# The last batch of a two-layer graph network: denominators by products, a new order on GpSimd, and an end row block by block

## The chip, the cores and the metric

One core of a Trainium2 chip (trn2) runs the whole program. The metric is the device time of one execution in microseconds (us). The kernel before took 3909.1 us, the median of three runs (3908.46 to 3909.31). The traces name the engines PE (TensorE, matrix products), PEld (its weight loads), DVE (VectorE), ACT (ScalarE), POOL (GpSimd) and SP (SyncE, which issues the transfers).

The change acts on the last 90 us of some 3904 us, so a time of one execution is a blunt tool: it also holds the luck of everything earlier. So beside the times I use three stretches of each trace:

- **start to sums**: from the start of the last batch's first scores product to the end of its last denominator product;
- **sums to statistic**: from there to the end of the last row's statistics on VectorE;
- **closing**: from there to the end of the span.

## The reference, cut to what matters

Two layers over 32 batches of 512 nodes with 512 features: a graph sum with layer norm, then masked attention with 8 heads of 64, an output projection and layer norm.

```python
x = _layernorm(x + _L0_gnn_ref(x, adj, W, b))                 # layer 0
q, k, v = split_heads(x @ Wq.T + bq), ...                     # layer 1
scores = jnp.where(adj == 0, -inf, einsum('bhqd,bhkd->bhqk', q, k) / 8)
attn = softmax(scores)                                        # divides by the row's sum: the denominator
out = einsum('bhqk,bhkd->bhqd', attn, v)
x = _layernorm(x + out @ Wo.T + bo)
```

## The kernel before

Batches are pipelined. Attention of batch b runs in eight steps, counted from 0 to 7 below, two for each of four pairs of heads; into each step the program puts pieces of other work (projections of batch b - 1, the next batch's layer 0). Each engine works through its own list in program order. For the last batch there is no next batch, so the steps are thin and waits show.

```python
def presum(hp, half):          # denominators: add the four blocks of masked exponentials
    if half == 0:
        ES[hp] = work([P, 2, N], "es", 1)
        nc.gpsimd.tensor_add(ES[hp], E[0], E[1])
    else:
        nc.vector.tensor_add(ES[hp], ES[hp], E[half])        # half = 2, 3: 1.22 us each or more

def sums(b, hp):               # then one product with ones for each head
    pl = ov_tile()
    for s in range(2):
        nc.tensor.matmul(pl[s*HD:(s+1)*HD, :], ones[:, :HD], ES[hp][:, s, :], start=True, stop=True)
    RL[hp] = (pl, work([P, N], "rl", 1))

def rest(b, hp):               # four reciprocals, scaling of the pair's values, a checksum (the "told sum")
    return [(invert, b, hp, c) for c in range(4)] + [(scale, b, hp), (tell, b, hp)]

def last_steps():              # the work put into the last batch's eight steps
    m = B - 2
    p = [pc("pj", m, i, bank) for i, bank in ALONE]          # seven pieces of m's output projection: 1,6,2,7,5,4,3
    c = [z(combos, TO, m, ot_quarter(m), (1, 2)), z(combos, TO, m, ot_quarter(m), (3, 4))]
    own = [(4 * GA, last_part, hp, 0) for hp in range(3)]    # the last batch's own projection, blocks 0 and 1
    return [[z(last_load), p[0], FLUSH] + c + [z(add_bo, B-1, 0), z(add_bo, B-1, 1)], [p[1], p[2]], [p[3], p[4]],
            [p[5], p[6], z(stats, m, 0), z(stats, m, 1)],
            [FLUSH, own[0], z(apply, m, 0), z(apply, m, 1), z(store, m)], [own[1]], [FLUSH, own[2]], []]

def last_part(hp, half):
    if hp == 0:
        if half == 0: ACC[0], ACC[1] = mm_tile("a"), mm_tile("b")
        else:
            t = sc_tile()
            ACC[2], ACC[3] = t[:, 0, :], t[:, 1, :]          # two halves of ONE tile
    ...                                                       # one product for each block of 128 rows

# the end row, after the eight steps
values(B - 1, HP - 1, 1)
sums(B - 1, HP - 1)
for hp in range(HP - 1): last_part(hp, 1)                     # blocks 2 and 3, pairs 0 to 2
for g in rest(B - 1, HP - 1): ...                             # reciprocals, scaling
for ic in range(2): last_part(HP - 1, ic)
tell(B - 1, HP - 1)
for ic in range(NC): last_rows(ic)                            # add, statistics, normalise, store
```

FLUSH means: issue here what is left of `rest`. Piece 1 leaves three additions for GpSimd; the combinations (differences of quarters of the attention's result) are GpSimd's too, and pieces 5, 6, 7 and 4 read them. A "piece" waits for its combination, and the values of one pair wait for the scaling of an earlier pair, which frees their PSUM buffer (a tile that holds results of TensorE). The masks, of which the texts speak, are VectorE's multiplications of the exponentials by the graph's edges.

## Time and profile before

| part of the trace of before | from | to | us |
|---|---|---|---|
| all that the change leaves alone | 0 | 3804.28 | 3804.28 |
| start to sums | 3804.28 | 3881.98 | 77.70 |
| sums to statistic | 3881.98 | 3894.41 | 12.43 |
| closing | 3894.41 | 3904.1 | 9.69 |

Only the last three rows can move. TensorE's waits in them are 0.47, 5.00, 2.17, 2.98, 4.22 and 1.40 us; the prediction shows the lines of the four longest. A trace line gives start, length, engine, line of the program, operation, output and inputs, shapes, and in square brackets the idle time ahead of it with what ended it.

### The profile page before, as it was taken

The numbers are of one execution on the slowest core, as the hardware profiler recorded it, in microseconds if no ns is written. First come the engines' busy times: TensorE is split into PE (matmuls) and PEld (weight loads), VectorE is DVE, ScalarE is ACT, GpSimd is POOL, SyncE is SP. The second block draws the span as 40 slices with busy tenths as digits, with TensorE's granted clock in tenths as the row PEclk, the third lists the DMA queues.
The fourth block names the chain that finished last, engine by engine and source line by source line (L and its number), as shares of the span: only waits on it lengthen the run. The fifth ranks groups of instructions, "written<-read, shape, count | busy, mean of one in ns | idle before, by whom it ended". The sixth has DMA issues, their size and how long they took to land.

```text
span 3904.1 us, 46897 instructions
## 1 busy us (share of the span) xinstructions
PE 3848.6 (99%) x17370; PEld 2639.9 (68%) x17370; DVE 2606.6 (67%) x3525; ACT 1057.8 (27%) x1476; POOL 1900.3 (49%) x1861
## 2 busy tenths in 40 slices
PE   9999999999999999999999999999999999999997
PEld 6666666766676666676667676667666667666763
DVE  4667676666666676666767666666667666666666
ACT  2222222222222222322222222222222232222222
POOL 4455554554544545445555355454454544555523
PEclk9999999999999999999999999999999999999998
DMA  7333333333334233333333332333433333333330
GB/s 251 116 109 100 114 108 116 120 91 110 114 108 124 87 116 111 111 119 111 97 114 110 114 122 90 111 113 109 123 90 113 114 108 120 114 95 112 111 106 23
DMA packets 281866, 433.88 MB, mean 111 GB/s; under 512 B 23072, under 2 KB 119840, under 8 KB 281632
## 3 DMA queue, kind: packets, MB, share of 16 engines
q1 hardware_dynamic: 281376, 430.27, 35.5%
q8 instruction: 142, 2.33, 0.2%
q14 instruction: 92, 0.75, 0.1%
q0 software_dynamic: 256, 0.53, 0.0%
HBM read 389.29 MB, written 41.42 MB: 110 GB/s over the span
## 4 chain that ended last, share of the span: by engine, by line
PE 76%; DVE 12%; POOL 9%; issue 2%; ACT 1%; DMA 0%; SPq 0%; POOLq 0%
PE mma L375 22%; PE mmb L375 22%; PE sc L427 10%; PE ov L448 9%; POOL xh L390 5%; PE mmb L299 3%; DVE rl L461 3%; PE mma L299 3%; PE ov L455 2%; DVE st L265 2%; DVE xh L393 2%; POOL big L344 2%; DVE e L432 2%; POOL es L438 2%; PE sc L292 2%
## 5 line engine op out<-in xcount | busy, mean ns | idle before, releaser
L432 DVE TENSOR_TENSOR e<-sc,edge 128x1024 f32<-128x1024 f32 x512 | 602.5, 1218 | 421.8 <-ACT sc L431 421.8
L431 ACT ACTIVATE sc<-sc 128x1024 f32<-128x1024 f32 x512 | 493.1, 1007 | 1276.0 <-PE sc L427 1275.7
L375 PE MATMUL mmb<-ring,big 128*128 128x256 f32 x3144 | 733.6, 382 | 8.2 <-POOL big L344 7.9
L375 PE MATMUL mma<-ring,big 128*128 128x256 f32 x3112 | 725.2, 381 | 4.3 <-POOL big L344 3.0
L375 PEld LDWEIGHTS mmb<-ring,big 128*128 128x128 f32 x3144 | 591.6, 190 | 131.9 <-DVE e L432 23.5
L375 PEld LDWEIGHTS mma<-ring,big 128*128 128x128 f32 x3112 | 583.9, 190 | 129.4 <-DVE e L432 25.2
L344 POOL TENSOR_TENSOR big<-big 128x512 f32<-128x512 f32 x376 | 549.5, 1488 | 220.1 <-DVE big L293 177.9
L184 POOL TENSOR_TENSOR xlo<-xh,xhi 128x512 fp32r<-128x512 f32 x128 | 200.6, 1577 | 738.2 <-ACT xhi L183 738.2
L427 PE MATMUL sc<-q,k 64*128 64x512 f32 x2048 | 509.7, 616 | 0.0
L448 PE MATMUL ov<-e,v 128*64 128x512 f32 x2048 | 497.1, 606 | 8.2 <-DVE oT L471 8.2
L461 DVE RECIPROCAL rl<-ov 128x128 f32<-128x128 f32 x512 | 462.6, 930 | 5.6 <-PE ov L455 1.8
L375 PE MATMUL mma<-big,ring 128*128 128x256 f32 x1808 | 433.1, 382 | 2.2 <-DVE xh L393 2.2
L375 PE MATMUL mmb<-big,ring 128*128 128x256 f32 x1776 | 425.3, 382 | 3.1 <-DVE xh L393 2.4
L267 POOL TENSOR_SCALAR mv<-mv 128x1 f32<-128x1 f32 x256 | 50.4, 197 | 740.5 <-DVE mv L266 730.4
L375 PEld LDWEIGHTS mma<-big,ring 128*128 128x128 f32 x1808 | 337.9, 190 | 80.6 <-issue 26.0
L438 POOL TENSOR_TENSOR es<-e 128x1024 f32<-128x1024 f32 x128 | 301.3, 2354 | 173.6 <-PE ov L455 172.3
L375 PEld LDWEIGHTS mmb<-big,ring 128*128 128x128 f32 x1776 | 332.0, 190 | 78.7 <-issue 24.3
L448 PEld LDWEIGHTS ov<-e,v 128*64 128x64 f32 x2048 | 124.7, 136 | 349.2 <-issue 274.2
L440 DVE TENSOR_TENSOR es<-es,e 128x1024 f32<-128x1024 f32 x256 | 353.4, 1380 | 0.1
L427 PEld LDWEIGHTS sc<-q,k 64*128 64x128 f32 x2048 | 176.5, 186 | 208.9 <-issue 207.0
L393 DVE TENSOR_TENSOR xh<-xh,mmb 128x512 f32<-128x512 f32 x186 | 125.8, 677 | 211.8 <-PE mmb L375 210.7
L390 POOL TENSOR_TENSOR xh<-xh,p 128x512 f32<-128x512 f32 x186 | 231.9, 1275 | 72.4 <-ACT sc L431 39.0
(141 smaller groups left out, 3688.1 us busy)
## 6 DMA issues: line engine op xcount, KB each, us to landing
ring<-wq SPq DMA_DIRECT2D x160, 256.0 KB, 2.6
ring<-wv SPq DMA_DIRECT2D x160, 256.0 KB, 2.6
ring<-wk SPq DMA_DIRECT2D x160, 256.0 KB, 5.4
ring<-wi SPq DMA_DIRECT2D x155, 256.0 KB, 2.6
ring<-wj SPq DMA_DIRECT2D x155, 256.0 KB, 2.7
ring<-wo SPq DMA_DIRECT2D x155, 256.0 KB, 2.6
xh<-in_x_dram SPq DMA_DIRECT2D x32, 1024.0 KB, 6.6
out_dram<-xh SPq DMA_DIRECT2D x31, 1024.0 KB, 5.2
```

Source lines behind the costliest of these rows:

```text
L299: nc.tensor.matmul(pm, parts[w][:, jc, :], adjR[:, jc, :], start=(w == 0 and jc == 0), stop=(w == 1 and jc == NC - 1))
L344: nc.gpsimd.tensor_tensor(dst, p, q, op=OP.subtract)
L375: nc.tensor.matmul(pm[:, c * Q:(c + 1) * Q], lhs, rhs, start=first, stop=(kc == 1 and n == len(terms) - 1), skip_group_check=True)
L390: nc.gpsimd.tensor_tensor(d, d, p1, op=OP.add)
L393: nc.vector.tensor_tensor(d, d, pm, op=OP.add)
L427: nc.tensor.matmul(ps[:, s, :], KT[b, hp // 2][r, hp % 2, kc * P:(kc + 1) * P], QT[b, hp // 2][r, hp % 2, :], start=True, stop=True)
L431: nc.scalar.activation(ps, ps, AF.Exp, scale=QSCALE)
L432: nc.vector.tensor_tensor(e, ps, edge[:, kc:kc + 1, :].to_broadcast([P, 2, N]), op=OP.mult)
L438: nc.gpsimd.tensor_add(ES[hp], E[0], E[1])
L440: nc.vector.tensor_add(ES[hp], ES[hp], E[half])
L448: nc.tensor.matmul(PV[hp][s * HD:(s + 1) * HD, :], V[b][:, kc, c0:c0 + HD], E[kc][:, s, :], start=(kc == 0), stop=(kc == NC - 1))
L461: nc.vector.reciprocal(rl[:, c], pl[:, c])
```

## The change

The intent, in three parts. **Order:** in the first step of the last batch, the denominator sum and the first combinations go ahead of the additions on GpSimd, piece 2 ahead of piece 6. **Products:** in the last batch, TensorE multiplies three things by ones and accumulates, so VectorE's two additions for each pair go away. **End row:** reciprocal, scaling and projection go block by block, with each block's row behind them.

```diff
+    def last_sums(hp, parts=(0, 2, 3)):
+        if 0 in parts:
+            RL[hp] = (ov_tile(), work([P, N], "rl", 1))
+        for kc in parts:
+            src = ES[hp] if kc == 0 else E[kc]
+            for s in range(2):
+                nc.tensor.matmul(RL[hp][0][s*HD:(s+1)*HD, :], ones[:, :HD], src[:, s, :], start=(kc == 0), stop=(kc == 3))
 ...
-        return [[z(last_load), p[0], FLUSH] + c + [z(add_bo, B-1, 0), z(add_bo, B-1, 1)], [p[1], p[2]], [p[3], p[4]], [p[5], p[6], z(stats, m, 0), z(stats, m, 1)],
-                [FLUSH, own[0], z(apply, m, 0), z(apply, m, 1), z(store, m)], [own[1]], [FLUSH, own[2]], []]
+        return [[z(last_load), FLUSH, c[0], p[1], c[1]], [p[2], p[6]], [p[5], p[7], z(add_bo, B-1, 0), z(add_bo, B-1, 1)],
+                [p[3], p[4], z(stats, m, 0), z(stats, m, 1)], [FLUSH, own[0], z(apply, m, 0), z(apply, m, 1), z(store, m)],
+                [own[1]], [FLUSH, own[2]], []]
 ...
-                    sums(b, ph)
+                    last_sums(ph) if b == B - 1 else sums(b, ph)
 ...
-            late = [(presum, hp, 0)] if half == 0 else [(presum, hp, 2), (presum, hp, 3)]
+            late = [(presum, hp, 0)] if half == 0 else [(presum, hp, 2), (presum, hp, 3)] if b < B - 1 else []
 ...
-    values(B - 1, HP - 1, 1)
-    sums(B - 1, HP - 1)
+    last_sums(HP - 1, (0,))
+    for kc in (2, 3):
+        values(B - 1, HP - 1, 1, (kc,))
+        last_sums(HP - 1, (kc,))
     for hp in range(HP - 1):
         last_part(hp, 1)
-    for g in rest(B - 1, HP - 1): ...
-    for ic in range(2):
-        last_part(HP - 1, ic)
+    for ic in range(NC):
+        invert(B - 1, HP - 1, ic)
+        scale(B - 1, HP - 1, slice(ic * P, (ic + 1) * P))
+        last_part(HP - 1, ic=ic)
+        if ic > 0:
+            last_rows(ic - 1)
     tell(B - 1, HP - 1)
-    for ic in range(NC):
-        last_rows(ic)
+    last_rows(NC - 1)
```

In the new list `p` is keyed by the piece's own number.

More of the change, by code (lines that the diff above doesn't have):

```diff
@@ L440, in presum, with values @@
             nc.vector.tensor_add(ES[hp], ES[hp], E[half])
-    def values(b, hp, half):
+    def values(b, hp, half, kcs=None):
         if half == 0:
             PV[hp] = ov_tile()
-        for kc in range(2 * half, 2 * half + 2):
+        for kc in kcs or range(2 * half, 2 * half + 2):
             for s in range(2):
@@ L456, in sums @@
         RL[hp] = (pl, work([P, N], "rl", 1))
+    def last_sums(hp, parts=(0, 2, 3)):
[4 more added lines that the diff above has]
+            for s in range(2):
+                nc.tensor.matmul(RL[hp][0][s * HD:(s + 1) * HD, :], ones[:, :HD], src[:, s, :], start=(kc == 0), stop=(kc == 3))
     def invert(b, hp, part):
@@ L466, in tell, with scale @@
         nc.vector.tensor_tensor_reduce(pl, pl, rl, 1.0, 0.0, OP.add, OP.add, told[:, j:j + 1])
-    def scale(b, hp):
+    def scale(b, hp, c=slice(0, N)):
         if hp % 2 == 0:
             OT[b, hp // 2] = work([P, 2, N], "oT", 3)
-        nc.vector.tensor_mul(OT[b, hp // 2][:, hp % 2, :], PV[hp], RL[hp][1])
+        nc.vector.tensor_mul(OT[b, hp // 2][:, hp % 2, c], PV[hp][:, c], RL[hp][1][:, c])
     def rest(b, hp):
@@ L634, in last_steps @@
         m = B - 2
-        p = [pc("pj", m, i, bank) for i, bank in ALONE]
+        p = {i: pc("pj", m, i, bank) for i, bank in ALONE}
         c = [z(combos, TO, m, ot_quarter(m), (1, 2)), z(combos, TO, m, ot_quarter(m), (3, 4))]
         own = [(4 * GA, last_part, hp, 0) for hp in range(3)]
-        return [[z(last_load), p[0], FLUSH] + c + [z(add_bo, B - 1, 0), z(add_bo, B - 1, 1)], [p[1], p[2]], [p[3], p[4]], [p[5], p[6], z(stats, m, 0), z(stats, m, 1)],
-                [FLUSH, own[0], z(apply, m, 0), z(apply, m, 1), z(store, m)], [own[1]], [FLUSH, own[2]], []]
+        return [[z(last_load), FLUSH, c[0], p[1], c[1]], [p[2], p[6]], [p[5], p[7], z(add_bo, B - 1, 0), z(add_bo, B - 1, 1)],
+                [p[3], p[4], z(stats, m, 0), z(stats, m, 1)], [FLUSH, own[0], z(apply, m, 0), z(apply, m, 1), z(store, m)],
+                [own[1]], [FLUSH, own[2]], []]
     def run(f):
@@ L649, in last_load, with last_part @@
         W["wo"] = [t[:, 0:2, :], t[:, 2:4, :]]
-    def last_part(hp, half):
+    def last_part(hp, half=None, ic=None):
         if hp == 0:
@@ L657, in last_part @@
                 ACC[2], ACC[3] = t[:, 0, :], t[:, 1, :]
-        for ic in range(2 * half, 2 * half + 2):
+        for ic in (range(2 * half, 2 * half + 2) if ic is None else (ic,)):
             nc.tensor.matmul(ACC[ic], OT[B - 1, hp // 2][:, hp % 2, ic * P:(ic + 1) * P], W["wo"][hp // 2][:, hp % 2, :],
@@ L723, in gnn_attention_kernel @@
             extra = []
-    values(B - 1, HP - 1, 1)
-    sums(B - 1, HP - 1)
+    last_sums(HP - 1, (0,))
+    for kc in (2, 3):
+        values(B - 1, HP - 1, 1, (kc,))
+        last_sums(HP - 1, (kc,))
     for hp in range(HP - 1):
         last_part(hp, 1)
-    for g in rest(B - 1, HP - 1):
-        if g[0] is not tell:
-            g[0](*g[1:])
-    for ic in range(2):
-        last_part(HP - 1, ic)
+    for ic in range(NC):
[4 more added lines that the diff above has]
+            last_rows(ic - 1)
     tell(B - 1, HP - 1)
-    for ic in range(NC):
-        last_rows(ic)
+    last_rows(NC - 1)
     flags()
```

## The prediction

> **What bounds the kernel now.** I read the page first: engines, clock row, chain of waits. All of it is one core running 32 batches.
>
> ```profile
> PE 3848.6 (99%) x17370; PEld 2639.9 (68%) x17370; DVE 2606.6 (67%) x3525; ACT 1057.8 (27%) x1476; POOL 1900.3 (49%) x1861
> PEclk9999999999999999999999999999999999999998
> ```
>
> TensorE is busy for 99% of the span and its clock falls in the last fortieth only. The diff acts on the last batch only (its conditions are `b == B - 1`, or code after the loop; the last period's list is its own), so nothing before about 3808 us of the 3904.1 us span should move. Ninety-odd us are in play, 2.4% of the span, and most of those are products that stay. Next I read that stretch as a timeline, by engine, and in windows. First its opening:
>
> ```profile
> 3811.62 3.72 POOL L390 TENSOR_TENSOR xh<-xh,p 128x512 f32<-128x512 f32 x3 [27.32 <-ACT p L382]
> 3815.31 2.33 POOL L438 TENSOR_TENSOR es<-e 128x1024 f32<-128x1024 f32 x1
> 3817.61 1.25 POOL L344 TENSOR_TENSOR big<-oT 128x512 f32<-128x512 f32 x1
> 3818.94 1.26 POOL L344 TENSOR_TENSOR big<-oT,big 128x512 f32<-128x512 f32 x1
> ...
> 3820.25 3.67 PE L375 MATMUL mmb<-ring,big 128*128 128x256 f32 x8 [5.00 <-POOL big L344]
> ```
>
> GpSimd works through three additions, a denominator sum and two combinations, in program order. Piece 6 of the output projection needs the second combination, so TensorE stands for 5.00 us, then runs its eight instructions in 3.67 us where the same group elsewhere takes 1.92. The windows (columns: stretch, its length, then busy time of PE, PEld, DVE, ACT, POOL, then clock, DMA share, GB/s) give the reason:
>
> ```profile
> 3820.00:3822.00 2.00, 1.75 (x4) 1.48 (x5) 0.00 (x0) 0.00 (x0) 2.00 (x3) 0.57 0.00 0
> 3834.00:3838.00 4.00, 1.86 (x8) 0.56 (x9) 3.96 (x6) 1.93 (x2) 0.00 (x0) 1.00 0.00 0
> 3855.00:3857.00 2.00, 1.90 (x6) 0.76 (x8) 2.00 (x4) 0.00 (x0) 0.00 (x0) 0.50 0.48 178
> 3870.00:3872.00 2.00, 2.00 (x4) 0.66 (x2) 0.00 (x0) 0.00 (x0) 0.00 (x0) 0.50 0.00 0
> ```
>
> After idle gaps of 5.00, 2.98 and 4.22 us the clock is half; after one of 2.17 us (in the second line) it is whole. The gaps come from one chain, here in TensorE's timeline with its idle time in brackets:
>
> ```profile
> 3838.03 1.94 PE L448 MATMUL ov<-e,v 128*64 128x512 f32 x8 [2.17 <-DVE oT L471]
> ...
> 3855.10 3.26 PE L448 MATMUL ov<-e,v 128*64 128x512 f32 x8 [2.98 <-DVE oT L471]
> ...
> 3869.14 2.07 PE L659 MATMUL mma<-xh,oT 128*128 128x512 f32 x2 [4.22 <-DVE oT L471]
> ```
>
> Sums on TensorE, then four reciprocals and the scaling on VectorE, then TensorE may go on. The end, from the chain of waits (start, length, what):
>
> ```profile
> 3879.53 1.23 DVE es L440
> 3880.77 0.14 issue
> 3880.90 1.08 PE ov L455 x4
> 3881.98 5.35 PE sc L659 x12
> 3887.33 0.87 PE mma L659 x2
> 3888.20 0.02 issue
> 3888.23 0.70 DVE xh L664
> ```
>
> From 3888.23 VectorE does four rows back to back; its last statistic ends at 3894.42. Small GpSimd operations, one activation, a store and the closing instructions fill the rest to 3904.1. VectorE's reciprocals (`L461`) are hidden behind the twelve products.
>
> **What the Trainium skill says.** "TensorE: Matmul & The Clock Gate", part 1: clock gated to half after an idle window of about 3.4 us, windows free-running. The trace agrees: the clock returns at about 3823.7, 3857.8 and 3874.9 (worked out from the means of my windows), which are 10 and 5 times 3.41 us apart. A window 33% busy lowered it (3851.0 to 3854.4), one 57% busy did not (3833.9 to 3837.3). "TensorEngine Tiling (Array Packing)", When to Use Tiling: with 64 columns of stationary operand two products share the array. It fits: two 128*64 sums over 512 columns take 0.86 to 0.88 us together, one 128*128 product over 512 columns 0.87 us alone. "VectorE: DVE Perf Modes", First, the fixed hardware budget: reciprocal is an iterated divide. The trace agrees that it is dear: 0.85 us for 128 columns in a run of four, as against 0.69 us for a multiplication over 512.
>
> **The change, part by part.** I lay the measured durations along the new program order. Units from the chain: scores 1.92, values 1.87, one product of the sums for a pair of heads 0.86, two pieces 1.92 + 1.74, an own pair 1.92, sums' end to scaled result seen by TensorE 4.20 (3.40 reciprocals, 0.70 scaling, waits 0.10). All starts below drop the 3800.
>
> 1. Order on GpSimd. The denominator sum now starts when its inputs and buffer are there (about 9.1), ends at 11.4; the first combination ends 12.7; the second waits for VectorE's scaling (ends 13.2) and ends 14.5; the three additions follow to 18.2. TensorE: values 13.31 to 15.18, piece 2 (wants only the scaled heads), piece 6, both done at 18.84, 2.5 us behind GpSimd. Before, they were done at 25.65. Gain 6.8: 5.0 of wait and 1.75 of half clock. The bias addition, 6.93 us, moves a step later, where GpSimd has nothing else.
>
> 2. Three products for one, step 2: two more at 0.86, cost 1.7. Shift 5.1.
>
> 3. Step 3 waits for the scaling as before. On VectorE the order (piece, reciprocal, piece, three reciprocals, scaling) is the same, so the 2.17 us gap stays: 0.
>
> 4. Step 4 costs another 1.7, but here VectorE was late: sums done at 48.3, reciprocals only at 50.84, because two additions at 1.22 us, the statistics and the masks were in its queue. Without the additions its masks end at 38.58 + 0.6 (piece) + 3.3 (statistics) + 2.3 (masks) = 44.8, TensorE's sums at 44.9. Values of step 5 start at 44.92 + 4.20 = 49.1, before 55.10. Shift 6.0, so this step gives 0.9 net. TensorE's own pair and scores fill to 48.7: a gap of 0.5 for 2.98.
>
> 5. With that gap gone the clock stays: 1.87 for 3.26. Gain 1.4, shift 7.4.
>
> 6. Step 6: 1.7 more of products, the gap of 4.2 stays, and the half clock behind it. Shift 5.65: values of step 7 at 70.2 for 75.82.
>
> 7. Last pair of heads: values 1.87, then five groups of four instructions at about 0.87, sums done at 76.4 (28 instructions, no wait). Before: 81.98, with 2.47 of additions in the way. The masks end at about 72.8, ahead of their use. Shift 5.6.
>
> 8. End row. The twelve products of the first three pairs are still ahead of the last pair's in TensorE's order, so the first row can be added no sooner than 6.25 after the sums (3888.23 less 3881.98), as before. In that wait VectorE now does only two blocks of reciprocal and scaling (2.4); then it stands at row 0, in order. Blocks 2 and 3 (0.87 + 0.30 each; the 0.30 is an estimate from 0.28 for a 128-column operation on VectorE) and the told sum (0.75) come between the rows. From first addition to last statistic: 1.63 + 3 x 1.52 + 2 x 1.17 + 0.75 = 9.3, before 6.19. Loss 3.1.
>
> Sum: 6.8 - 1.7 + 0 + (2.6 - 1.7) + 1.4 - 1.7 - 0.1 - 3.1 = 2.5 us gained. The closing stretch is unchanged. 3909.1 - 2.5 = 3906.6.
>
> **The rivals.** (a) The block-by-block end pays as intended: then the 5.6 of point 7 survive, perhaps with a us more, 3902.5 to 3903.5. Against it: the twelve products hold the first row, and VectorE had idle time there which it now spends waiting in order; for it only that the stores start earlier and spread out. (b) The products cost more than they free: 6.9 us more of TensorE, and the first wait only moves to another operation (the additions, now late on GpSimd, holding VectorE's addition of piece 6). Then 3909 to 3911. Against it: piece 6 needs only the first addition, done at 15.8, and comes at 18.8. (c) The clock falls in another place. The gap of step 3 was just short of it; with the windows otherwise placed a gap of 2.2 lies all in one window of 3.41 with some 40 to 50% chance (an estimate from the 33 and 57% above), costing up to 1.7. Where the gap of step 6 lies decides whether half clock lasts one window or two: 1.2 either way. This is luck for each execution: 3905 to 3908.5.
>
> **Range and chances.** I take 3906.6. Luck of the windows is plus or minus 1.5, the end row plus or minus 1, so 3904.8 to 3908.3 eight times in ten, with rival (a) the likelier miss. All rivals are within 0.2% of the time before; 2% is 78 us, more than the stretch's waits together. Faster by 2%: 0.005, within 2%: 0.99, slower: 0.005.
>
> **What would show it.** Right: piece 2 straight behind the values near 3815, no wait for GpSimd's combination, clock whole there; step 5's wait under 1 us and its values at 1.9; twelve instructions for the sums at 2.6; a VectorE wait of about 3.5 between the second scaling and the first row's addition, then reciprocals between the rows and 9.3 us to the last statistic. Wrong: a new long wait in steps 1 to 3, half clock behind step 3, or a last statistic less than 7.5 us after the first row's addition.

## The result, and the profile after

The changed kernel took 3904.77 us, the median of four runs (3903.31 to 3906.64); before, with one run more, 3908.78 (3904.76 to 3909.31). The ratio is 0.9992, 95% interval 0.9975 to 1.001. By that interval the two cannot be told apart by their times alone. The traces can: the span went from 3904.1 to 3901.5 us, and the parts are

| part | before | after | gain | foretold |
|---|---|---|---|---|
| up to the last batch | 3804.28 | 3803.72 | 0.56 | 0 |
| start to sums | 77.70 | 72.02 | 5.68 | 5.6 |
| sums to statistic | 12.43 | 17.68 | -5.25 | -3.1 |
| closing | 9.69 | 8.08 | 1.61 | 0 |

The whole page hardly changes; its first line, which answers to the one of before, shows only 32 more matrix instructions:

```profile
PE 3853.7 (99%) x17402; PEld 2641.4 (68%) x17402; DVE 2595.7 (67%) x3520; ACT 1057.0 (27%) x1476; POOL 1909.7 (49%) x1861
```

The opening of the last batch in the timeline of after, GpSimd first, then TensorE:

```profile
3808.52 2.35 POOL L438 TENSOR_TENSOR es<-e 128x1024 f32<-128x1024 f32 x1 [24.79 <-PE ov L455]
3810.83 1.27 POOL L344 TENSOR_TENSOR big<-oT 128x512 f32<-128x512 f32 x1
3812.74 1.28 POOL L344 TENSOR_TENSOR big<-oT,big 128x512 f32<-128x512 f32 x1 [0.64 <-DVE oT L480]
3813.97 3.74 POOL L390 TENSOR_TENSOR xh<-xh,p 128x512 f32<-128x512 f32 x3
...
3825.38 4.95 POOL L326 TENSOR_TENSOR xh<-xh,bo_r 128x512 f32<-128x512 f32 x4
```

```profile
3812.74 1.94 PE L448 MATMUL ov<-e,v 128*64 128x512 f32 x8 [0.47 <-DVE oT L480]
3814.61 1.99 PE L375 MATMUL mma<-ring,oT 128*128 128x256 f32 x8
3816.44 1.89 PE L375 MATMUL mmb<-ring,big 128*128 128x256 f32 x8
```

Piece 2 and piece 6 follow the values without a bracket, so without a wait, and both take 1.9 us: whole clock. The second combination starts when VectorE's scaling is there and ends at 3814.0, 2.4 us ahead of its use. The waits that were 2.17, 2.98 and 4.22 us are now:

```profile
3832.43 1.94 PE L448 MATMUL ov<-e,v 128*64 128x512 f32 x8 [2.17 <-DVE oT L480]
...
3848.69 1.94 PE L448 MATMUL ov<-e,v 128*64 128x512 f32 x8 [0.48 <-DVE oT L480]
...
3863.12 2.08 PE L669 MATMUL mma<-xh,oT 128*128 128x512 f32 x2 [4.22 <-DVE oT L480]
```

The middle one has gone with the half clock behind it (3.26 us before, 1.94 now). Then the end row, VectorE and TensorE:

```profile
3877.97 0.29 DVE L480 TENSOR_TENSOR oT<-ov,rl 128x128 f32<-128x128 f32 x1
3881.98 0.69 DVE L674 TENSOR_TENSOR xh<-xh,mma 128x512 f32<-128x512 f32 x1 [3.72 <-PE mma L669]
...
3887.20 0.29 DVE L480 TENSOR_TENSOR oT<-ov,rl 128x128 f32<-128x128 f32 x1
3889.65 0.69 DVE L674 TENSOR_TENSOR xh<-xh,sc 128x512 f32<-128x512 f32 x1 [2.17 <-PE sc L669]
```

```profile
3884.84 1.48 PE L669 MATMUL sc<-xh,oT 128*128 128x512 f32 x2 [2.04 <-DVE oT L480]
3887.54 2.08 PE L669 MATMUL sc<-xh,oT 128*128 128x512 f32 x2 [1.22 <-DVE oT L480]
```

VectorE stands 3.72 us at row 0, as the prediction said, and then again 2.17 us at row 2, as it did not. Row 2's own product began at 3884.84 and was long done at 3889.65; what ended just then (3887.54 + 2.08) is the product of block 3. The two blocks are halves of one tile. Block 3's product ran at half clock (the granted clock was 0.50 from 3886 to 3890): 2.08 us, where a product at whole clock takes 1.02. Last, the closing stretch. SyncE's waits, before and after (who waited for whom, us in total, times, longest):

```profile
SPq L869 <- PEq L869: 2.3, 2, 2.0
```

```profile
SPq L881 <- PEq L881: 0.4, 2, 0.2
```

The closing barriers of the program wait 2.0 us for TensorE's instruction stream in one kernel and not in the other, though no line of the closing code was touched.

### The profile page after: what moved, and what is told of

It reads as the page before. It is cut to its first block, busy times and chain, and to the rows that moved or that the text cites. A ratio compares the mean times of both kernels' runs of the same rounds, so it can differ in the third digit from the quotient of the medians.

```text
span 3901.5 us, 46958 instructions
## 1 busy us (share of the span) xinstructions
PE 3853.7 (99%) x17402; PEld 2641.4 (68%) x17402; DVE 2595.7 (67%) x3520; ACT 1057.0 (27%) x1476; POOL 1909.7 (49%) x1861
## 4 chain that ended last, share of the span: by engine, by line
PE 77%; DVE 12%; POOL 8%; issue 2%; ACT 1%; DMA 0%; SPq 0%
PE mma L375 23%; PE mmb L375 23%; PE sc L427 10%; PE ov L448 9%; POOL xh L390 5%; PE mmb L299 3%; DVE rl L470 3%; PE mma L299 3%; PE ov L455 2%; DVE xh L393 2%; DVE st L265 2%; POOL big L344 2%; DVE e L432 2%; POOL es L438 2%; PE sc L292 2%
## 5 line engine op out<-in xcount | busy, mean ns | idle before, releaser
L440 DVE TENSOR_TENSOR es<-es,e 128x1024 f32<-128x1024 f32 x248 | 341.6, 1377 | 0.0
L393 DVE TENSOR_TENSOR xh<-xh,mma 128x512 f32<-128x512 f32 x186 | 125.6, 676 | 213.1 <-PE mma L375 213.1
```

Of the source, the lines that this page charges most:

```text
L393: nc.vector.tensor_tensor(d, d, pm, op=OP.add)
```

## The experiments

Eleven kernels ran, all with correct results, each timed over five rounds beside the kernel before. The table gives all of them; "ratio" is to before. The first two rows are the kernels of the change, with the traces shown above. The stretches of a kernel come from one traced execution each. Where two kernels share an end row, sums to statistic agrees: 12.42 or 12.43 us in all five with the old one.

| kernel | median us | before, same rounds | ratio (95%) | start to sums | sums to statistic | closing |
|---|---|---|---|---|---|---|
| before | | | | 77.70 | 12.43 | 9.69 |
| changed | 3904.77 | 3908.78 | 0.9992 (0.9975 to 1.001) | 72.02 | 17.68 | 8.08 |
| e1_old_end | 3900.85 | 3908.34 | 0.9982 (0.9968 to 0.9995) | 72.15 | 12.42 | 8.25 |
| e2_own_tiles | 3903.23 | 3908.34 | 0.9987 (0.9973 to 1.0001) | 72.34 | 15.54 | 8.00 |
| e3_order_alone | 3900.24 | 3908.34 | 0.9978 (0.9964 to 0.9992) | 71.14 | 12.43 | 9.60 |
| e4_products_alone | 3906.74 | 3908.34 | 0.9997 (0.9984 to 1.0011) | 79.11 | 12.42 | 8.06 |
| e5_end_alone | 3913.73 | 3908.81 | 1.0012 (0.9998 to 1.0025) | 78.67 | 17.69 | 9.80 |
| e6_gap_filled | 3899.80 | 3908.81 | 0.9977 (0.9963 to 0.999) | 65.93 | 17.38 | 8.12 |
| e8_warm | 3903.58 | 3908.81 | 0.9985 (0.9971 to 0.9999) | 71.11 | 17.68 | 8.48 |
| e7_all | 3893.03 | 3908.81 | 0.9958 (0.9944 to 0.9971) | 64.20 | 11.56 | 8.49 |
| e9_longer | 3904.62 | 3907.37 | 0.9993 (0.998 to 1.0007) | 75.51 | 12.42 | 8.25 |
| e10_all_vector_sums | 3890.87 | 3907.37 | 0.9956 (0.9943 to 0.997) | 61.70 | 11.56 | 10.31 |
| e11_all_mixed | 3888.74 | 3907.37 | 0.9951 (0.9938 to 0.9965) | 61.38 | 11.56 | 8.05 |

In the texts below, "stretch" is the sum of the first two parts (before 90.13 us, after 89.70 us).

**The old end row behind the new rest.**

```diff
-    for ic in range(NC):
-        invert(...); scale(..., block ic); last_part(HP - 1, ic=ic)
-        if ic > 0: last_rows(ic - 1)
-    tell(B - 1, HP - 1)
-    last_rows(NC - 1)
+    (the end row of before: all reciprocals, scaling, products, told sum, four rows)
```

> The changed kernel with the end row of before (all four reciprocals and the scaling first, then the last pair's products, then four rows). Measure: the stretch from the first scores product of the last batch's first step to the end of the last statistic (before: 3804.28 to 3894.42, 90.1 us; after: 3803.72 to 3893.42, 89.7 us), and in it the time from the end of the last denominator product to the last statistic (before 12.4 us, after 17.7 us). Theory (VectorE waits in order at row 0 and then has two blocks still to do between the rows; the end row costs more than it gives): 12.4 us again, stretch 84.4, time about 5 us under the changed kernel, 3899 to 3901. Rival (the end row pays, or costs nothing, and the long end of after is bad luck of the clock): 15 us or more, stretch 87 or more, time within 2 us of the changed kernel.

Sums to statistic came back to 12.42 us, the stretch was 84.57 and the time 3900.85 us. Its VectorE timeline shows the four reciprocals in one run of 3.39 us, hidden behind the twelve products, and a wait of 1.41 us at row 0 in place of 3.72. The block-by-block end costs 5.3 us; the rival falls.

**Blocks 2 and 3 in tiles of their own.**

```diff
-                t = sc_tile()
-                ACC[2], ACC[3] = t[:, 0, :], t[:, 1, :]
+                ACC[2], ACC[3] = sc_tile()[:, 0, :], sc_tile()[:, 0, :]
```

> The changed kernel with blocks 2 and 3 of the last projection in two PSUM tiles in place of two halves of one. Theory (row 2 waits for block 3's product because the wait is kept per tile): the 2.17 us wait of VectorE ahead of row 2's addition goes, from last denominator product to last statistic 15.5 us in place of 17.7, stretch 87.5, time 2.2 us under the changed kernel. Rival (row 2 waits because block 2's own product runs at half clock): a wait of over 1 us stays and the stretch is 89 or more.

Sums to statistic 15.54 us, stretch 87.88. VectorE's timeline has row 2 straight behind the last scaling, no bracket:

```profile
3893.01 0.29 DVE L480 TENSOR_TENSOR oT<-ov,rl 128x128 f32<-128x128 f32 x1
3893.22 0.68 DVE L673 TENSOR_TENSOR xh<-xh,sc 128x512 f32<-128x512 f32 x1
```

Block 3's product was as slow here (2.08 us) and nobody waited for it on row 2's behalf. So the 2.17 us came from the shared tile: the wait was on the last product written to the tile, not on the half that is read. The half clock stretched that product: at whole clock about 1.1 us of the 2.17 would have been left (an estimate: 2.17 less 2.08 plus 1.02). The times agree in direction only (3903.23, runs from 3901.13 to 3906.87): 2 us is within the spread of the runs.

**The new order alone.**

```diff
 kernel before, with only:
-        [z(last_load), p[0], FLUSH] + c + [z(add_bo, ...)...], [p[1], p[2]], [p[3], p[4]], [p[5], p[6], ...], ...
+        [z(last_load), FLUSH, c[0], p[1], c[1]], [p[2], p[6]], [p[5], p[7], z(add_bo, ...)...], [p[3], p[4], ...], ...
```

> The kernel before with only the new order of the last period's steps (combinations ahead of the additions on GpSimd, piece 2 ahead of 6). Theory (this is the part that gives, the other two cost): TensorE's 5.0 us wait and the half clock behind it go, everything later keeps its shape: stretch 83.3 (90.1 less 6.8), time 6 to 7 us under before, and so under the whole change. Rival (VectorE, which still adds the denominators, takes over the wait in steps 1 and 2 or at step 4): stretch 86 or more.

Start to sums 71.14 us in place of 77.70: 6.56 gained, 6.8 foretold. The stretch is 83.57, the time 3900.24 us, 8.1 under before of the same rounds (6 to 7 foretold; what goes beyond the stretch's 6.56 the trace does not explain). The order alone does better than the whole change. The wait of 5.0 us is gone; the waits of 2.17, 2.98, 4.22 and 1.40 us are all there as in before. VectorE did not take the wait over.

**The products alone.**

```diff
 changed kernel, with the last batch's step list and the end row of before
```

> The kernel before with only the three products in place of VectorE's sums (last pair's interleaved with its values, as in the change), old order and old end row. Theory (1.7 us more of TensorE for each of four pairs against the VectorE time freed in step 4, the clock kept in step 5 and the additions saved at the last pair): stretch 91.3, from 90.5 to 92, so a small loss; 5.0 us wait of step 1 still there. Rival (VectorE's sums were the bound and the products are the gain of the change): stretch 88 or less.

Start to sums 79.11 us, 1.41 more than before; stretch 91.53. TensorE still waits for the combination:

```profile
3820.79 3.78 PE L375 MATMUL mmb<-ring,big 128*128 128x256 f32 x8 [5.02 <-POOL big L344]
```

The products are a small loss in this part: 1.41 us, where the prediction's points 2 and 4 to 7 sum to 1.2. The closing stretch is 1.63 us shorter (see the run on the program's length below), so the two nearly cancel. The time, 3906.74 us, is 1.6 us under before; by its interval it cannot be told from before.

**The end row alone.**

```diff
 kernel before, with only the block-by-block end row (and the block arguments of scale and last_part)
```

> The kernel before with only the block-by-block end row. Theory (in-order waiting at row 0, then 2 blocks, the told sum and the shared-tile wait between the rows): from last denominator product to last statistic 17.7 us in place of 12.4, stretch 95.4 in place of 90.1, time 5 us over before. Rival (the end row is neutral by itself): stretch 91 or less.

Sums to statistic 17.69 us against 12.43, time 3913.73 us, 4.9 over before: the end row costs 5.26 us by itself. The stretch, 96.36, came out 1 us over what I expected; the rest of that is in start to sums (78.67 for 77.70), where no line was changed. Its windows put the clock at 0.55 and 0.60 behind the 2.17 us gap of step 3, where in before it was whole: the rival (c) of the prediction, met here by chance. It cost 1.65 us there. The half clock behind the 5.0 us wait lasted 0.6 us longer, too; but behind the 2.99 us gap of step 5 the clock stayed whole, which gave 1.3 back.

Each read in the stretch on which it acts, the three parts by themselves make -6.56, +1.41 and +5.26, together +0.1 us; the whole change makes -0.43 in the same stretch.

**The gap of step 6 filled with own work.**

```diff
-                [own[1]], [FLUSH, own[2]], []]
+                [], [FLUSH, own[1]], [own[2]]]
```

> The changed kernel with the own products of pairs 1 and 2 moved one step later, so that pair 1's products and the scores of step 7 run in the 4.2 us in which TensorE waits for the scaling of pair 2. Theory (the gap and the half clock behind it are on the path): wait under 1 us, clock whole in step 7, stretch 83.9 in place of 89.7, time 5 to 6 us under the changed kernel. Rival (the time comes back in VectorE's masks of step 7 or in the end row): stretch 87 or more.

The wait of 4.22 us is 0.48, start to sums 65.93 in place of 72.02, stretch 83.31, time 3899.80 us. The gap and its clock were on the path; nothing came back later.

**The same gap filled with work whose result nobody reads.**

```diff
-                [own[1]], [FLUSH, own[2]], []]
+                [own[1]], [FLUSH, z(warm), own[2]], []]
+    def warm():
+        t = sc_tile()
+        for j in range(4):
+            nc.tensor.matmul(t[:, j % 2, :], ones, W["wo"][0][:, 0, :], start=True, stop=True)
```

> The changed kernel with four idle-work products (result unread) in the same 4.2 us gap, so the wait stays as long but TensorE is busy in it. It measures the clock alone. Theory (half clock behind the gap costs as measured there: 3.8 for 1.9 us of own products and 2.7 for 1.9 us of scores): own products and scores at whole clock, stretch 87.1 in place of 89.7. Rival (the later work hides it, behind the masks of VectorE): stretch 89 or more.

The stretch was 88.79, not 87.1. By its number that is nearer the rival, so I looked where it was lost, in TensorE's timeline of this run:

```profile
3834.34 2.54 PE L448 MATMUL ov<-e,v 128*64 128x512 f32 x8 [2.17 <-DVE oT L480]
3836.82 3.03 PE L375 MATMUL mma<-ring,oT 128*128 128x256 f32 x8
...
3866.68 1.12 PE L674 MATMUL mma<-xh,oT 128*128 128x512 f32 x2 [0.59 <-DVE oT L480]
```

Behind the same 2.17 us gap as ever the clock went to half in this execution, and the values of step 5 came 46.62 us after the batch's start in place of 44.97: 1.65 us lost, in a part that this kernel shares with the changed one. From the values of step 5 to the sums it took 24.49 us, against 27.05: 2.56 gained, 2.6 expected (89.7 less 87.1). So the half clock behind the gap of 4.2 us cost 2.6 us, and that behind a gap of 2.17 us cost 1.65 us in some executions and nothing in others.

**A version of all gains.**

```diff
-        [p[5], p[7], z(add_bo, B-1, 0), ...], [p[3], p[4], z(stats, ...)...], ..., [own[1]], [FLUSH, own[2]], []
+        [p[5], p[7], FLUSH, p[3], z(add_bo, B-1, 0), ...], [p[4], z(stats, ...)...], ..., [], [FLUSH, own[1]], [own[2]]
+    (blocks 2 and 3 in tiles of their own, as above)
+    for hp in range(HP - 2): last_part(hp, 1)
+    for g in rest(B - 1, HP - 1): g[0](*g[1:])
+    last_part(HP - 1, 0)
+    for ic in (2, 3): last_part(HP - 2, ic=ic); last_part(HP - 1, ic=ic)
+    for ic in range(NC): last_rows(ic)
```

> All that the theory says should help: new order and products, own products moved into the gap of step 6, piece 3 moved behind the reciprocals of step 2, blocks 2 and 3 in own tiles, and an end row with all reciprocals, scaling and told sum first, then blocks 0 and 1 of the last pair ahead of the remaining products. Theory: stretch 89.7 - 5.9 (gap of step 6 and its clock) - 1.7 (gap of step 3) - 6.4 (end row: first row 5.1 us after the sums, 11.3 in place of 17.7) = 75.7; time 3890 to 3893, faster than both. If the parts collide (VectorE bound in steps 5 to 7): 79 or more.

Stretch 75.76 us, 75.7 foretold; time 3893.03 us (3890 to 3893 foretold). The waits of TensorE up to the sums are now 0.44 to 0.48 us.

**The length of TensorE's instruction stream.** The closing stretch fell by 1.6 us with the products and with nothing else. "Runtime: NRT & Kernel Launch" of the Trainium skill, Instruction fetch mechanics, says that an engine's instructions are fetched in blocks of 16 KiB and that a taken branch to a target outside the present blocks waits for a fetch. The program ends with a branch over its general path. So I lengthened the stream of the kernel before by as many instructions as the change adds.

```diff
 kernel before, with
-    [own[1]], [FLUSH, own[2]], []
+    [own[1]], [FLUSH, z(extra_pe), own[2]], []
+    def extra_pe():
+        t = sc_tile()
+        for j in range(16):
+            nc.tensor.matmul(t[0:32, j % 2, 0:64], ones[:, 0:32], W["wo"][0][:, 0, 0:64], start=True, stop=True)
```

> The kernel before with 16 tiny products more (result unread; 32 matrix and 32 weight-load instructions, as many as the change adds on TensorE) in TensorE's 4.2 us gap of step 6. It is about the closing stretch, from the last statistic to the end of the span: 9.7, 9.6 and 9.8 us in the three kernels without the three products, 8.0 to 8.5 in the six with them. Theory (it hangs on how many instructions TensorE's stream holds, not on what they do): closing stretch 8.0 to 8.5. Rival (it hangs on the products or on the new order of the end): 9.7.

Closing 8.25 us in place of 9.69, and the 2.0 us wait for TensorE's stream is 0.2:

```profile
SPq L874 <- PEq L874: 0.4, 2, 0.2
```

So it hangs on how many instructions the stream holds, not on the change's idea. The version with mixed sums (below), which adds half as many, has the short closing too (8.05). The traces show where the time goes. First the instructions of TensorE's queue around the end of before, then of after (duration in ns, first and last start):

```profile
L739 PEldq COMPARE_BRANCH  x1: 3780/3780/3780, 3896.3 to 3896.3; - x1
L869 PEldq DRAIN  x2: 8/8/8, 3900.3 to 3903.9; - x2
L869 PEldq EVENT_SEMAPHORE  x2: 51/51/51, 3903.8 to 3904.1; - x2
```

```profile
L751 PEldq COMPARE_BRANCH  x1: 4012/4012/4012, 3895.3 to 3895.3; - x1
L881 PEldq DRAIN  x2: 8/8/8, 3899.5 to 3901.0; - x2
L881 PEldq EVENT_SEMAPHORE  x2: 51/51/51, 3900.8 to 3901.5; - x2
```

The branch itself takes 3.4 to 4.3 us on TensorE in all thirteen traces (0.045 to 0.072 on the other engines), so it is not what got shorter. In the four kernels with the short stream TensorE then stands a second time, for 3.3 to 3.4 us: in before between 3900.3 and 3903.8. With VectorE's sums in the version of all gains (below) TensorE has one instruction more on record than in before, and this second stop comes one instruction earlier, so at the same count from the start. A stop at a fixed place in the stream fits a block border and the page; the fetch itself no trace shows. By chance the lengthened kernel shows the clock again: its gap of step 6 shrank to 2.31 us, the clock stayed whole there, and start to sums fell to 75.51.

**VectorE's sums in the version of all gains.**

```diff
-                    last_sums(ph) if b == B - 1 else sums(b, ph)
+                    sums(b, ph)
 (and late, and the last pair, as in the kernel before)
```

> The version of all gains, but with VectorE's sums in place of the three products for every pair. Theory (products cost TensorE 1.7 us a pair, give back 2.6 in step 4 and keep the clock in step 5): stretch 74.6 in place of 75.8, from 74 to 76. Rival (with the gaps filled VectorE has become the bound, and its sums come on the path): stretch 78 or more.

Start to sums 61.70, against 64.20 with the products; stretch 73.26, better than I had expected (74.6, from 74 to 76). With the gaps filled TensorE is the scarce engine, and VectorE's sums show up as one wait of 2.51 us in step 4, with half clock behind it (two blocks take 2.08 and 1.75 us for 1.13 and 1.02), which cost another 1.6. The closing stretch is back at 10.31.

**The sums mixed.**

```diff
-                    sums(b, ph)
+                    last_sums(ph) if b == B - 1 and ph == 1 else sums(b, ph)
 (pair 3 by products too)
```

> The version of all gains, with VectorE's sums for pairs 0 and 2 and the three products for pairs 1 and 3, where VectorE is late. Theory: 1.7 us of TensorE saved at pair 0, about 0.9 at pair 2 (there VectorE's masks come later), stretch 73.2, time 2 to 3 us under the version of all gains. Rival (VectorE's additions delay the masks of the next step by as much): stretch 75 or more.

Stretch 72.94, time 3888.74 us (3888.36 to 3888.94): the best of all, 18.6 us or 0.5% under before of the same rounds. Against the version with VectorE's sums throughout, though, only 0.32 us of its 2.1 us come from the mixing; 2.26 us are the closing stretch (8.05 against 10.31), that is, the length of the instruction stream. The 0.32 us leans on the half clock in the other version's one trace, 1.6 us; so whether mixing gains by itself stays open. TensorE's timeline of its end row: the first line is blocks 2 and 3 of pairs 0 and 1, which fill the wait for the scaling; the next two are blocks 0 and 1 of the last pair, so that row 0 can start; what is left runs behind them, beside VectorE's rows.

```profile
3867.42 3.70 PE L668 MATMUL sc<-xh,oT 128*128 128x512 f32 x8
3871.70 1.13 PE L668 MATMUL mma<-xh,oT 128*128 128x512 f32 x2 [0.59 <-DVE oT L480]
3872.67 1.02 PE L668 MATMUL mmb<-xh,oT 128*128 128x512 f32 x2
3873.53 3.60 PE L668 MATMUL sc<-xh,oT 128*128 128x512 f32 x8
```

## Why the prediction was right or wrong

It foretold a gain of 2.5 us and a time of 3906.6, range 3904.8 to 3908.3. The span fell by 2.6 us. The median of the four runs, 3904.77, lies 0.03 us under the range, the ratio times 3909.1 us gives 3906.0, inside it. The class, within 2%, was right. But the near match of 2.5 and 2.6 is luck: the stretch that the prediction is about gained 0.43 and not 2.5, and two things that it did not foresee, 1.61 in the closing stretch and 0.56 before the last batch, made up for it. Point by point, starts from the last batch's first scores product, and the shift at each:

| point of the prediction | before | after | shift | foretold |
|---|---|---|---|---|
| 1, scores of step 2 | 21.30 | 14.54 | 6.76 | 6.8 |
| 2, scores of step 3 | 29.59 | 24.55 | 5.04 | 5.1 |
| 4, values of step 5 | 50.82 | 44.97 | 5.85 | 6.0 |
| 5, scores of step 6 | 55.92 | 48.75 | 7.17 | 7.4 |
| 6, values of step 7 | 71.47 | 65.79 | 5.68 | 5.65 |
| 7, sums done | 77.70 | 72.02 | 5.68 | 5.6 |
| 8, row 0's addition | 83.95 | 78.26 | 5.69 | 5.6 |
| 8, last statistic | 90.13 | 89.70 | 0.43 | 2.5 |

- **Points 1 to 7 held**, each to 0.3 us, and the parts run alone bear them out: the order gives 6.6 and the products lose 1.4. Point 3 held too: the gap of step 3 is 2.17 us in both. (A slip without effect: the bias addition moved two entries later, not one; it took 4.95 us there, not 6.93.)
- **Point 8 was right in its mechanism and short in its size.** VectorE did wait in order at row 0 (3.72 us, some 3.5 foretold), and rows and blocks did then follow each other. The term that was mis-sized is "from first addition to last statistic ... 9.3": it measured 11.4 (3881.98 to 3893.42). What it lacked is the wait of row 2 for block 3's product, 2.17 us, which the tile of its own took away. I had read in the program that both blocks lie in one tile and not asked what a wait on it means.
- **"The closing stretch is unchanged" failed** in the other direction, by 1.61 us, for a reason outside the change's idea; the lengthened kernel before shows it.
- The remaining 0.56 us of the span's 2.6 came before the last batch began, where the programs do the same work: luck.
- **Rival (a)**, the end row pays, fell: it costs 5.3 us. **Rival (b)**, the products cost more than they free and the wait moves, fell in its second half and holds in its first: 1.4 us of loss alone, 2.5 in the version with the gaps filled. **Rival (c)**, luck of the clock behind the 2.17 us gap, did not strike the changed kernel's trace, but did strike two of the ten traces with that gap, at 1.65 us, as large as foretold (up to 1.7); the chance had been put at 40 to 50%. The traces' clock records tell the two cases apart: counted from one change of the clock, all others of the last batch fall on a grid of 3.41 us. Of its windows at whole clock, each with TensorE busy for 43% or less halved the clock, none with 44% or more did. Behind the 2.17 us gap the two that fell had 36 and 38%; the eight that held had 44 to 64%.

So in the stretch only the new order of the lists is a gain among the three parts; the end row gave most of it back, and the products' shorter closing is a side effect of the program's length. Leaving out the end row alone (3900.85) or keeping the order alone (3900.24) would each have given more.

## What to carry to other kernels

When every engine works through one list in order, splitting a stage into blocks helps only if, unlike here, the consumer's list does not put a wait for block 0 ahead of the producer's work on block 2; ask what the engine would have done in the wait. A gap of a few us on TensorE costs its length and can cost the half clock behind it (1.3 to 2.6 us here), so move useful work into it, even work that belongs a step later. Judge a change in the last 2% of a program by stretches of the trace: the time of an execution also holds the luck of the clock and of where the instruction stream ends.

## What the Trainium skill lacked or had wrong

- "TensorE: Matmul & The Clock Gate", HAM oscillation: it gives "no PE-idle gaps >~3.4µs" as the rule. Here a gap of 2.17 us halved the clock in two of ten traces, costing 1.65 us, one of 2.51 us in the one trace that has it, and one of 2.98 us in the kernel before, while one of 2.99 us in the run of the end row alone did not. A window need not be idle: worked out from the clock records of the thirteen traces, windows of 3.41 us with up to 43% of busy time halved the clock and those from 44% did not (for example 1.25 us busy of 3.42 in the run with unread work, and 1.51 of 3.42 with the products alone).
- "Runtime: NRT & Kernel Launch", Instruction fetch mechanics: it names the wait after a taken branch and gives no size, nor that the end of a program changes with the length of the stream. Here the branch took 3.4 to 4.3 us on TensorE, a second stop of 3.3 to 3.4 us followed in the kernels with the short stream, and 64 instructions more on TensorE (32 matrix and 32 weight-load instructions) took 1.4 us off the end of the kernel before (9.69 to 8.25 us). That the fetch is the cause is not shown.
- "VectorE: DVE Perf Modes": it says how a reciprocal is made and gives no time for one. Four of 128 columns took 3.39 us, 6.6 ns a column, where a multiplication over 512 took 0.69 us.
- No page says that a wait may be kept for a whole PSUM tile when only half of it is read (that is the program's doing, not the chip's): 2.17 us here.
